# The begin of a two-layer kernel: sums of squared weights by wide products, and fewer projections ahead of the first scores

## The chip, the cores and the metric

The kernel runs on one core of one Trainium2 chip. Its time is device microseconds (us) of one execution. Three runs of the kernel before took 6031.06, 6007.41 and 6010.15 us; the median is 6010.15. A fourth execution, the one that the profile shows, took 6021.71 us.

A core has five engines with queues of their own: PE (TensorE, the matrix engine, with its weight loads shown as PEld), DVE (VectorE), ACT (ScalarE), POOL (GpSimd) and SP (SyncE, which here only issues transfers). Sixteen DMA engines move data.

## What is computed

The input x has 8 sequences of 1024 tokens with 512 values. Two residual layers follow each other. The change is in the first, modulated attention with 16 heads of 32 values:

```python
def _dcoef(weight, style):
    return rsqrt(einsum('oi,bi->bo', square(weight), square(style)) + EPS_DM)
...
x = x * s1[:, None, :]                       # s1, s2: the two halves of the styles
x = (x - mean(x)) * rsqrt(var(x) + EPS_IN)
q_dc, k_dc, v_dc = (_dcoef(w, s1) for w in (q_weight, k_weight, v_weight))
w_dc, u_dc = (_dcoef(w, s2) for w in (w_weight, u_weight))
q = heads(x @ q_weight.T * q_dc); k = heads(x @ k_weight.T * k_dc)
v_flat = x @ v_weight.T * v_dc * s2
attn = softmax(q @ k.T * d ** -0.5)
out = (attn @ heads(v_flat)) @ w_weight.T * w_dc + v_flat @ u_weight.T * u_dc
```

So each of the five weight matrices (512 x 512) needs, for each of the 8 sequences and each of 512 outputs, a factor: the root of a sum over inputs of squared weight times squared style, inverted. Only q and k factors are needed for scores; v's factor is needed for the weighing, w's and u's for the two output projections.

The second layer is a gated state-space scan over 1024 steps with 16 states for each of 1024 channels. The change touches it only in how a few tiles are allotted.

## The kernel before, in words

**Layout.** All data are float32. The attention is cut into 32 blocks: 8 sequences b by 4 groups o of four heads (128 output columns). A block has 16 slots: 8 groups of 128 queries by 2 pairs of heads. The main loop (L326 to L393) runs over the 512 slots and two more. The order of instructions on each engine is the order of the program text (`manual_schedule`); nothing is reordered by a planner, and only semaphores make engines wait for each other.

**A slot.** `scores` (L243) makes two score tiles of 128 queries by 1024 keys: for the first half of the keys from qT and kT (L252), for the second half from q2 and k2 (L255). q2 and k2 are copies of q and of the second half of k in which the upper and lower 64 partitions are exchanged (`moved`, L176: two transfers on SP's queue), so that four products run in four row strips. DVE takes the negated maximum over keys (L360), ACT the exponential with its row sum (L370), DVE the reciprocal and POOL scales the probabilities (L375, L384, L389). In the next slot PE flips them in groups of four transposes (`flip`, L262); ACT copies the flips of the first head out (L367), DVE those of the second (L381, L386). Every second slot begins with `weigh` (L269), which multiplies the flipped probabilities of the two slots before with vt, the turned v, in four column strips.

**Background.** Between these steps the slot runs a number of pieces of a generator, `background(n)`: above all `project` for the next block (for each half of the tokens: v, k, the turn of v into vt, q; each projection is a chain of four products of 128x512, L153, one piece each), the turning of the next sequence's x, and the output projections `out_w` and `out_u` of sequences and blocks already done. PIECES (L322) says how many pieces each block has to spread over its 16 slots: 42, 42, 30 and 62. Block 0 of the first sequence has no `out_w`, so it has only the 26 pieces of `project`. A second generator, `aside`, loads and normalises the next sequence's x.

**The begin.** Ahead of the main loop the text runs, in this order:
1. L104 to L110: load both halves of x of sequence 0 with their styles (`load_x`: 1 MB and 256 KB each on SP's queue), `normalise` both (POOL multiplies by the style, L72; DVE takes mean and variance, L76 and L77; ACT the root, L79; DVE the reciprocal, L80 and L81; POOL scales, L86), then `turn` both (groups of four transposes on PE, L96, copied out by ACT and DVE in turn, L98 and L100).
2. L113 to L136: for each of q, k, v, w, u load the whole matrix (1 MB, L118) into one of two buffers, square it on ACT (L119, 128x2048), and form the sums with the squared weights as the stationary operand and the 8 squared styles as the moving one (L124): 16 products with 8 moving columns for each matrix. DVE adds a constant (L131). After all five, one root (L132), one reciprocal (L133), and two more factors (L135, L136).
3. L284 to L287: load the first block's slices of the q, k and v weights, run all of `project` for block 0 (24 products and 8 transposes), and issue the loads for block 1.

PSUM gives `ps_m` two buffers (tag "mm"), shared by projections, turns, sums of squares and weighing. ACT holds one table of functions at a time; the root and the exponential are in different ones, and a load shows as ACT_TABLE_LOAD.

**After the attention**, `gated_scan` allots its tiles in the space that the attention's pools leave, loads its weights on SP's queue, and runs a plan of steps by number. `load_x1` fetches a 512 KB chunk of the first layer's result into one of two x1 buffers; `fetch` broadcasts rows from DRAM into xb buffers (256 KB each, 2048 transfers).

Of the kernel before, what the change touches and what calls it, by code (L numbers as in the profile page):

```python
# [16 lines left out]
B = 8  # L17
# [14 lines left out]
def modulated_attention(ctx, tc, const, x1_d, xu_d, S, x, xT, cond, wT, ident, sT):  # L32
# [15 lines left out]
    eps = const.tile([P, 1], F32, name="eps_h")  # L48
    nc.vector.memset(eps, EPS)
    dc = const.tile([P, 5, KH, B], F32, name="dc")  # L50
# [5 lines left out]
    def load_x(b, hf):  # L56

        xq = tok.tile([P, 4, H], F32, name="xq")
        nc.sync.dma_start(
            out=xq, in_=x[b, hf * HW : (hf + 1) * HW].rearrange("(j p) c -> p j c", p=P)  # L60
        )
        sr = tok.tile([P, H], F32, name="sr")
        nc.sync.dma_start(out=sr, in_=cond[b, 0:H].unsqueeze(0).to_broadcast([P, H]))
        return xq, sr

    def normalise(xs):
# [4 lines left out]
        for j in range(4):  # L71
            nc.gpsimd.tensor_mul(xq[:, j], xq[:, j], sr)  # L72
            yield
# [11 lines left out]
        for j in range(4):  # L85
            nc.gpsimd.tensor_scalar(xq[:, j], xq[:, j], rs[:, j, 0:1], rs[:, j, 1:2], ALU.mult, ALU.add)  # L86
            yield
# [14 lines left out]

    xh_now = []
    first = [load_x(0, 0), load_x(0, 1)]  # L104
    for xs in first:
        for _ in normalise(xs):
            pass
    for xs in first:
        for _ in turn(xs, xh_now.append):
            pass  # L110


    with tc.tile_pool(name="w0", bufs=2) as wp:  # L113
        s2T = wp.tile([P, 2 * KH, B], F32, name="s2T")
        nc.scalar.activation(s2T, sT, AF.Square)
        for n, name in enumerate(NAMES):
            w = wp.tile([P, KH, H], F32, name="w")
            nc.sync.dma_start(out=w, in_=wT[name].rearrange("(k p) o -> p k o", p=P))  # L118
            nc.scalar.activation(w, w, AF.Square)  # L119
            off = 0 if n < 3 else KH  # L120
            d_ps = ps_m.tile([P, KH, B], F32, tag="mm", name="mm_ps")
            for o in range(KH):
                for k in range(KH):
                    nc.tensor.matmul(  # L124
                        d_ps[:, o, :],
                        w[:, k, o * P : (o + 1) * P],
                        s2T[:, off + k, :],
                        start=(k == 0),
                        stop=(k == KH - 1),
                    )  # L130
            nc.vector.tensor_scalar_add(dc[:, n], d_ps, EPS_DM)  # L131
        nc.scalar.activation(dc, dc, AF.Sqrt)  # L132
        nc.vector.reciprocal(dc, dc)  # L133
    qdc, kdc, vdc, wdc, udc = (dc[:, n] for n in range(5))
    nc.vector.tensor_scalar_mul(qdc, qdc, float(HD) ** -0.5)  # L135
    nc.vector.tensor_mul(vdc, vdc, sT[:, KH : 2 * KH, :])  # L136
# [21 lines left out]

    def load_w(name, o):
# [6 lines left out]
    def project(ws, xh, b, o, st):  # L166

        qT = st["q"] = ring.tile([P, S], F32, tag="qT", name="qT")
        kT = st["k"] = ring.tile([P, S], F32, tag="kT", name="kT")
        q2 = st["q2"] = ring.tile([P, S], F32, tag="q2", name="q2")  # L170
        k2 = st["k2"] = ring.tile([P, HW], F32, tag="k2", name="k2")
        vT = st["v"] = ring.tile([P, S], F32, tag="vT", bufs=5, name="vT")
        for hf in range(2):
            c = half(hf)

            def moved(dst, src):  # L176
                nc.sync.dma_start(out=dst[64:128], in_=src[0:64])
                nc.sync.dma_start(out=dst[0:64], in_=src[64:128])
# [13 lines left out]
            for name, out in (("v", v_out), ("k", k_out), ("q", q_out)):  # L192
                yield from chain([(ws[name][:, k], xh[hf][:, k]) for k in range(KH)], out)
                if name == "k":
                    if hf == 0:
                        vt = st["vt"] = ring.tile([P, KT, P], F32, tag="vt", name="vt")
                    ps = ps_m.tile([P, 4, P], F32, tag="mm", name="mm_ps")
                    for j in range(4):
                        nc.tensor.transpose(ps[:, j], vT[:, (4 * hf + j) * P : (4 * hf + j + 1) * P], ident)
                    nc.scalar.copy(vt[:, 4 * hf : 4 * hf + 4], ps)  # L200
                    yield
# [82 lines left out]
    fetch_w(0)  # L284
    for _ in project(wts[0], xh_now, 0, 0, sts[0, 0]):
        pass
    fetch_w(1)  # L287

    def background(n):
# [5 lines left out]
        if o == KH - 1:  # L295
            w0 = load_w("u", 0)
        if o < KH - 1:
# [8 lines left out]
        fetch_w(n + 2)  # L306
        if o < 2 and b > 0:
# [18 lines left out]
    for n in range(len(slots) + 2):  # L326
# [10 lines left out]
        if bo is not None:  # L337

            done, pieces = n % SB + 1, PIECES[bo[1]]
            few = max(1, (pieces - 2 * NQ + NQ) // SB)  # L340
            due = few * (done - done // 2) + -(-(pieces - NQ * few) * (done // 2) // NQ) - ran
            ran += due
# [56 lines left out]
def gated_scan(ctx, tc, const, x1_d, S, w_in, w_conv, cols, ln_g, ln_b, w_x, w_xd, w_dt, b_dt, a_log,  # L399
# [33 lines left out]
    def load_chunk(c):  # L433
        x1 = two.tile([P, KH, B, TC], F32, name="x1")
# [10 lines left out]
    lg = load(cols["ln_g"], "lg", [P, KI])  # L445
# [544 lines left out]
```

## Time and profile before

| What | Value |
|---|---|
| Median of three runs | 6010.15 us (6007.41 to 6031.06) |
| Profiled execution | 6021.71 us |
| Its span, first to last instruction | 6019.9 us |
| Begin, to the first maximum over scores (L360) | 98.96 us |
| Block 0, from its first scores (L252) to those of block 1 | 97.74 to 199.3 us |
| Attention ends, last outputs stored (L232) | about 3464 us |
| Scan, first broadcast (L771) to the end | 3530 to 6020 us |
| PE, DVE, ACT, POOL busy | 94%, 74%, 64%, 26% |
| Mean granted TensorE clock | 0.98 of full |

"Busy" for PE is modelled from pipelined instructions; a PE that is busy may still run at a reduced clock, so the granted clock (PEclk, as a share of full speed) has to be read beside it. A product of float32 operands appears as two PE records, a transpose as one. A line of the timeline or of a table of groups names line, engine, operation, output and inputs, then how often; in brackets follows the idle time before it and what ended it. A line of the chain of waits gives start, length and what the end of the program waited for at that time.

### The profile page before, as it was taken

What the parts mean: (1) busy time and instruction counts of PE and PEld (TensorE: products, weight loads), DVE (VectorE), ACT (ScalarE), POOL (GpSimd) and SP (SyncE); (2) the same over time, 40 slices, a digit from 0 to 9 for tenths busy, and PEclk for the clock granted to TensorE, in tenths of its full rate; (3) what the DMA queues carried; (4) which work ended last, traced back from release to release, by engine and by line L of the source; (5) the groups of instructions that cost most, each with busy time, mean ns of one, the idle gap of its engine ahead of it and who ended that gap; (6) DMA issues with size and microseconds to landing.
All of it is one profiled execution on the core that took longest, in us unless ns stands there. A gap on an engine that the chain in (4) does not pass through costs nothing.

```text
span 6019.9 us, 113426 instructions
## 1 busy us (share of the span) xinstructions
PE 5660.1 (94%) x42960; PEld 3310.4 (55%) x42960; DVE 4469.2 (74%) x6917; ACT 3846.8 (64%) x6743; POOL 1549.8 (26%) x1668
## 2 busy tenths in 40 slices
PE   7999999999999999999999879999999999999998
PEld 5555555555555555555555545555555555555553
DVE  2666666766666666667666569999989998989997
ACT  3655555655655555556555358877777777777786
POOL 2433433433433434334333201101111111111111
PEclk8999999999999999999999989999999999999999
DMA  2102212111112022121111279999989999899997
GB/s 71 38 17 64 52 41 64 29 57 50 37 48 66 21 59 59 34 64 37 51 37 36 63 203 252 248 244 248 249 239 246 248 250 243 241 242 247 241 249 207
DMA packets 387648, 781.81 MB, mean 130 GB/s; under 512 B 203664, under 2 KB 285840, under 8 KB 354336
## 3 DMA queue, kind: packets, MB, share of 16 engines
q1 hardware_dynamic: 358432, 756.07, 46.2%
q0 software_dynamic: 28672, 18.48, 1.4%
q8 instruction: 342, 5.60, 0.4%
q14 instruction: 202, 1.65, 0.1%
HBM read 663.62 MB, written 83.89 MB: 124 GB/s over the span
## 4 chain that ended last, share of the span: by engine, by line
PE 51%; DMA 27%; DVE 8%; ACT 8%; SPq 4%; issue 2%; POOL 0%; ACTq 0%; DVEq 0%; POOLq 0%
DMA xb<-xd 24%; PE mm_ps L153 16%; PE t_ps L262 13%; PE s_ps L252 9%; PE mm_ps L269 8%; DVE h L805 4%; SPq L771 4%; ACT pr L370 3%; ACT pT L367 2%; PE in_ps L546 1%; DMA xd<-xt 1%; ACT xb L781 1%; DVE xt L604 1%; PE y_ps L792 1%; PE o_ps L744 1%
## 5 line engine op out<-in xcount | busy, mean ns | idle before, releaser
L360 DVE TENSOR_REDUCE nmax<-s_ps 128x1 f32<-128x1024 f32 x1024 | 1206.1, 1220 | 478.2 <-PE s_ps L255 477.6
L367 ACT COPY pT<-t_ps 128x512 f32<-128x512 f32 x1024 | 550.1, 589 | 1377.7 <-PE t_ps L262 1377.4
L805 DVE CUSTOM_DVE_ANT_0 h<-h,xb,lim 128x1024 f32<-128x1024 f32 x1024 | 1372.9, 1341 | 64.4 <-ACT xb L781 21.0
L262 PEld LDWEIGHTS t_ps<-ident,pr 128*128 128x128 f32 x8192 | 910.0, 141 | 647.0 <-issue 451.3
L781 ACT ACTIVATE xb<-xb,ws 128x1024 f32<-128x1024 f32 x1024 | 1152.4, 1146 | 174.6 <-DMA xb<-xd 151.8
L370 ACT ACTIVATE pr<-s_ps,nmax 128x1024 f32<-128x1024 f32 x1024 | 1140.3, 1128 | 5.7 <-DVE nmax L360 5.5
L262 PE MATMUL t_ps<-ident,pr 128*128 128x128 f32 x8192 | 1095.9, 277 | 30.8 <-ACT pT L367 28.5
L546 PE MATMUL in_ps<-x,win 128*128 128x256 f32 x2048 | 530.2, 405 | 88.0 <-DMA x<-x_d 88.0
L389 POOL TENSOR_SCALAR pr<-pr,rinv 128x1024 f32<-128x1024 f32 x512 | 575.2, 1123 | 144.7 <-DVE rinv L388 140.8
L252 PE MATMUL s_ps<-kT,qT 32*128 32x512 f32 x2048 | 601.0, 641 | 4.4 <-ACT pr L370 4.4
L255 PE MATMUL s_ps<-k,q 32*128 32x512 f32 x2048 | 578.0, 640 | 0.0
L759 POOL DMA_DIRECT2D out<-o_sb x256 | 150.5, 594 | 1642.5 <-ACT xr L557 824.3
L375 POOL TENSOR_SCALAR pr<-pr,rinv 128x1024 f32<-128x1024 f32 x256 | 287.5, 1123 | 1107.8 <-PE t_ps L262 740.2
L269 PEld LDWEIGHTS mm_ps<-pT,vt 128*32 128x32 f32 x16384 | 438.0, 110 | 235.3 <-issue 94.4
L269 PE MATMUL mm_ps<-pT,vt 128*32 128x128 f32 x16384 | 517.5, 274 | 47.7 <-ACT vt L200 18.6
L792 PE MATMUL y_ps<-h,yw 128*32 128x512 f32 x4096 | 533.5, 610 | 12.4 <-DVE h L805 12.4
L546 PEld LDWEIGHTS in_ps<-x,win 128*128 128x128 f32 x2048 | 397.6, 200 | 248.9 <-issue 120.1
L384 POOL TENSOR_SCALAR pr<-pr,rinv 128x1024 f32<-128x1024 f32 x256 | 287.5, 1123 | 880.8 <-DVE rinv L383 854.0
L704 PE MATMUL g_ps<-win,x1t 128*128 128x512 f32 x1024 | 467.3, 599 | 2.3 <-ACT sq_ps L630 2.3
L744 PE MATMUL o_ps<-wout,xt 128*128 128x512 f32 x1024 | 463.7, 596 | 0.1
L566 DVE SCALAR_TENSOR_TENSOR xc<-xr,cw,xc 128x256 f32<-128x256 f32 x768 | 369.5, 481 | 94.6 <-ACT xc L559 81.4
L381 DVE COPY pT<-t_ps 128x512 f32<-128x512 f32 x512 | 352.1, 688 | 77.2 <-PE t_ps L262 76.8
(131 smaller groups left out, 6830.7 us busy)
## 6 DMA issues: line engine op xcount, KB each, us to landing
xb<-xd SPq DMA_DIRECT2D x2048, 256.0 KB
xd<-xt SPq DMA_DIRECT2D x64, 512.0 KB
xq<-in_x SPq DMA_DIRECT2D x16, 1024.0 KB
q<-qT SPq DMA_DIRECT2D x128, 128.0 KB
xr<-in_xT SPq DMA_DIRECT2D x64, 256.0 KB
xu_d<-xr SPq DMA_DIRECT2D x64, 256.0 KB
xr<-xu_d SPq DMA_DIRECT2D x64, 256.0 KB
x_d<-xr SPq DMA_DIRECT2D x64, 256.0 KB
```

What stands on the lines that cost most here:

```text
L153: nc.tensor.matmul(ps, w, x, start=(k == 0), stop=(k == KH - 1))
L252: nc.tensor.matmul(s_ps[i][:, 0:HW], st["q"][r, qc], st["k"][r, 0:HW], start=True, stop=True)
L255: nc.tensor.matmul(s_ps[i][:, HW:S], st["q2"][r, qc], st["k2"][r], start=True, stop=True)
L262: nc.tensor.transpose(ps[:, j], pr[:, c0 : c0 + P], ident)
L269: nc.tensor.matmul(av[r], vt[:, kt, r], pT[:, i, kt], start=(kt == 0), stop=(kt == KT - 1), skip_group_check=True,)
L360: nc.vector.tensor_reduce(nmax[i], s_ps[i], AX.X, ALU.max, negate=True)
L367: nc.scalar.copy(pT[:, 0, 4 * g : 4 * g + 4], t_ps[g])
L370: nc.scalar.activation(fresh[i], s_ps[i], AF.Exp, bias=nmax[i], accum_out=rsum[i])
L546: nc.tensor.matmul(ps, win_sb[:, kk, k * P : (k + 1) * P], st["x1"][:, kk].rearrange("p b t -> p (b t)"), start=(kk == 0), stop=False,)
L781: nc.scalar.mul(xbs[n], xbs[n], sts[c]["ws"][:, t : t + 1])
L792: nc.tensor.matmul(st["y", i][32 * r : 32 * r + 32, hf * 512 : (hf + 1) * 512], yws[i][:, 4 * q + r, :], hs[4 * g + r][:, hf * 512 : (hf + ...
L805: nc.vector._custom_dve(dve_ops.TENSOR_ADD_SAT, out=h, in0=last["h"], in1=xbs.pop(n), s0=lim[:, 0, t : t + 1], s1=lim[:, 1, t : t + 1],)
```

## The change

It has four parts.

1. **Sums of squares.** `demod` replaces the loop at L113. For each matrix ACT squares four blocks of 128x512 one by one; the squared styles, padded with zeros to 32 columns, are now the stationary operand, and each squared block is the moving one. The four blocks' products go to four strips of 32 partitions of one PSUM tile, side by side, and are not accumulated. DVE copies the tile out, PE turns it with four transposes, and DVE reduces over the four strips (128x32) and adds the constant. Root, reciprocal and the extra factors follow for each call of `demod`.
2. **Order of the begin.** Loads: the first half of x in two parts with its style between them, the whole k matrix, the second half, the slices of k and q, the whole q matrix. Then: normalise the first half, turn it, normalise the second, `demod` of k, turn the second half, `demod` of q. Only k (both halves) and q (first half) of block 0 are projected ahead of the scores; the four squares of v's matrix are issued too. The rest of block 0's work goes into its own background: the rest of `demod` of v, projections of v, both turns of v, q's second half, then block 1's projections as before, then `demod` of w and u. In this block 56 pieces are spread, six in each of the first three slots.
3. **First normalise.** For sequence 0 the product with the style is on DVE, and two of four scalings are on ACT instead of POOL.
4. **Tiles.** The pool "w0" is gone; whole matrices use buffers of "two" (tag pT) and "tok" (tag xq). sT, eps and dc move to a pool "own" that ends with the attention. In the scan x1 has three buffers instead of two, p_add one instead of two, and the loads of lg, lb and wdt and the column of zeros use tiles that exist anyway.

```diff
 def load_x(b, hf):
     xq = tok.tile([P, 4, H], F32, name="xq")
-    nc.sync.dma_start(
-        out=xq, in_=x[b, hf * HW : (hf + 1) * HW].rearrange("(j p) c -> p j c", p=P)
-    )
+    src = x[b, hf * HW : (hf + 1) * HW].rearrange("(j p) c -> p j c", p=P)
+    if b == 0:
+        nc.sync.dma_start(out=xq[:, 0:2], in_=src[:, 0:2])
+    else:
+        nc.sync.dma_start(out=xq, in_=src)
     sr = tok.tile([P, H], F32, name="sr")
     nc.sync.dma_start(out=sr, in_=cond[b, 0:H].unsqueeze(0).to_broadcast([P, H]))
+    if b == 0:
+        nc.sync.dma_start(out=xq[:, 2:4], in_=src[:, 2:4])
...
-            nc.gpsimd.tensor_mul(xq[:, j], xq[:, j], sr)
+            (nc.vector if first else nc.gpsimd).tensor_mul(xq[:, j], xq[:, j], sr)
...
-            nc.gpsimd.tensor_scalar(xq[:, j], xq[:, j], rs[:, j, 0:1], rs[:, j, 1:2], ALU.mult, ALU.add)
+            if first and j % 2 == 0:
+                nc.scalar.activation(xq[:, j], xq[:, j], AF.Identity, bias=rs[:, j, 1:2], scale=rs[:, j, 0:1])
+            else:
+                nc.gpsimd.tensor_scalar(xq[:, j], xq[:, j], rs[:, j, 0:1], rs[:, j, 1:2], ALU.mult, ALU.add)
...
+    s2T = own.tile([P, 2 * KH, HD], F32, name="s2T")
+    nc.vector.memset(s2T, 0.0)
+    nc.scalar.activation(s2T[:, :, 0:B], sT, AF.Square)
...
+    def demod(ns, ws):
+        for n, w in zip(ns, ws):
+            for k in range(KH):
+                nc.scalar.activation(w[:, k], w[:, k], AF.Square)
+                yield
+            off = 0 if n < 3 else KH
+            d_ps = ps_m.tile([P, H], F32, tag="mm", name="mm_ps")
+            for k in range(KH):
+                nc.tensor.matmul(
+                    d_ps[k * HD : (k + 1) * HD], s2T[:, off + k], w[:, k], start=True, stop=True,
+                    skip_group_check=True,
+                )
+            nc.vector.tensor_copy(w[:, 0], d_ps)
+            yield
+            t_ps = ps_m.tile([P, KH, P], F32, tag="mm", name="mm_ps")
+            for o in range(KH):
+                nc.tensor.transpose(t_ps[:, o], w[:, 0, o * P : (o + 1) * P], ident)
+            nc.vector.tensor_reduce(
+                dc[:, n], t_ps.rearrange("p o (k m) -> p o m k", k=KH)[:, :, 0:B], AX.X, ALU.add
+            )
+            nc.vector.tensor_scalar_add(dc[:, n], dc[:, n], EPS_DM)
+            yield
+        part = dc[:, ns[0] : ns[-1] + 1]
+        nc.scalar.activation(part, part, AF.Sqrt)
+        nc.vector.reciprocal(part, part)
...
-    fetch_w(0)
-    for _ in project(wts[0], xh_now, 0, 0, sts[0, 0]):
-        pass
+    first = [load_x(0, 0)]
+    full = {"k": load_full("k", two, "pT")}
+    first.append(load_x(0, 1))
+    wts[0] = {name: load_w(name, 0) for name in "kq"}
+    full["q"] = load_full("q", two, "pT")
+    demods = {name: demod((n,), (full[name],)) for n, name in ((1, "k"), (0, "q"))}
+    for part in (
+        normalise(first[0], True), turn(first[0], xh_now.append), normalise(first[1], True), demods["k"],
+        turn(first[1], xh_now.append), demods["q"],
+    ):
+        for _ in part:
+            pass
+    wts[0]["v"] = load_w("v", 0)
+    demods["v"] = demod((2,), (load_full("v", tok, "xq"),))
+    for _ in project(wts[0], xh_now, 0, 0, sts[0, 0], (("k", 0), ("k", 1), ("q", 0))):
+        pass
+    for _ in range(KH):
+        next(demods["v"])
     fetch_w(1)
...
+        if n == 0:
+            yield from demods["v"]
+            yield from project(
+                wts[0], xh_now, 0, 0, sts[0, 0], (("v", 0), ("v", 1), ("t", 0), ("t", 1), ("q", 1))
+            )
+            rest = [load_full(name, tok, "xq") for name in "wu"]
...
         fetch_w(n + 2)
+        if n == 0:
+            yield from demod((3, 4), rest)
...
-            done, pieces = n % SB + 1, PIECES[bo[1]]
+            done, pieces = n % SB + 1, PIECES[bo[1]] if n >= SB else 56
...
+            if n < 3:
+                due = 6
+            due = max(due, 0)
...
-        x1 = two.tile([P, KH, B, TC], F32, name="x1")
+        x1 = two.tile([P, KH, B, TC], F32, bufs=3, name="x1")
...
-        add = two.tile([P, NX], F32, name="p_add")
+        add = one.tile([P, NX], F32, name="p_add")
```

## The prediction, made before the changed kernel was run

> **What bounds the kernel now.** I read the slices of the page first: TensorE is near 9 tenths in slices 2 to 23 (attention, 151 us each), and from slice 24 on the DMA engines are at 9 (the scan). The change touches the first 200 us, so I asked for the busy table of windows there.
>
> ```profile
> core 0: us, PE busy (x) PEld busy (x) DVE busy (x) ACT busy (x) POOL busy (x), PEclk, DMA share, GB/s
> 20.00:40.00 20.00, 12.74 (x64) 10.74 (x62) 6.72 (x15) 6.28 (x8) 6.85 (x8) 0.89 0.00 0
> 40.00:60.00 20.00, 19.07 (x90) 18.97 (x90) 0.39 (x2) 4.44 (x3) 0.00 (x0) 0.50 0.48 158
> 60.00:80.00 20.00, 14.25 (x48) 10.48 (x48) 1.81 (x5) 2.31 (x3) 0.00 (x0) 0.59 0.14 39
> 100.00:120.00 20.00, 15.31 (x64) 7.47 (x64) 8.55 (x15) 8.66 (x16) 4.47 (x4) 0.83 0.18 49
> ```
>
> TensorE looks busy from 40 to 60 us, but at a granted clock of 0.50 and with nothing beside it. The chain of waits (start, length, what) says what that work is.
>
> ```profile
> 9.09 4.93 POOL xq L72 x4
> 18.92 4.91 POOL xq L72 x4
> 33.66 5.42 PE mm_ps L124 x32
> 39.15 5.61 DMA w<-in_wvT
> 44.87 1.92 ACT w L119
> 46.83 7.01 PE mm_ps L124 x32
> 53.89 5.38 DMA w<-in_wuT
> 61.34 7.01 PE mm_ps L124 x32
> 69.37 3.67 DMA w_v<-in_wvT
> 73.39 8.61 PE mm_ps L153 x16
> 94.11 3.71 PE mm_ps L153 x8
> 100.94 3.61 DMA w_v<-in_wvT
> ```
>
> From 33.7 to 73.4 us everything waits for the five sums of squares (L124) and for weights that two buffers let in late; then six projection chains run before the first score; then the next block's weights are awaited, 5.81 us of idle TensorE. Last, rows of the timeline: the first maximum over scores, and the starts of the scores of four slots.
>
> ```profile
> 98.96 2.35 DVE L360 TENSOR_REDUCE nmax<-s_ps 128x1 f32<-128x1024 f32 x2 [28.53 <-PE s_ps L255]
> 147.15 0.70 PE L252 MATMUL s_ps<-kT,qT 32*128 32x512 f32 x2
> 160.15 0.70 PE L252 MATMUL s_ps<-kT,qT 32*128 32x512 f32 x2
> 171.76 0.70 PE L252 MATMUL s_ps<-kT,qT 32*128 32x512 f32 x2
> 182.96 0.70 PE L252 MATMUL s_ps<-kT,qT 32*128 32x512 f32 x2
> 263.14 1.28 ACT L79 ACT_TABLE_LOAD   x1
> ```
>
> A pair of slots without background pieces takes 182.96 - 171.76 = 11.2 us, one with about 5 pieces 160.15 - 147.15 = 13.0; in block 3 (62 pieces, 7.75 a pair) pairs are 14.7 apart (the weighings at 3316.52 and 3331.22). A piece is one 128x512 product, 0.86 us at full clock (3.60 us for the chain of four at 78.39). So in block 0 a hidden piece costs 0.35 to 0.7 us, not nothing.
>
> **Part 1: the begin, up to the first maximum (98.96 before).** I walk the new order with rows of before.
> - First half of x: 0.5 MB less lies ahead of its styles, about 1.3 us at the 390 GB/s of 9 to 15 us, so they land near 7.6 instead of 8.94; its second part near 9.0. Four DVE products of 128x512 (1.22 us for 128x1024 at L717, so 0.63) end at 10.4. Four statistics (0.69 + 0.18 + gaps) take 3.7: 14.05. Root, reciprocal and product took 15.71 - 14.96 = 0.75: 14.8. ACT and POOL now share the scaling, two each (0.57 and 0.76): 16.5. Sixteen transposes in groups of four 0.95 to 1.0 apart (copies at 29.28, 30.13, 31.07, 32.03) and the last copy: 20.6. Before, POOL alone did the products at 1.23 each.
> - Second half: its data were there by 17. DVE products 2.5, statistics 3.7, root 0.75: 27.6; scaling 28.9; four squares of the keys' weights on ACT (1.85 for 128x2048 at L119; 0.56 each) to 31.1. The four 32-wide products run in four column strips; in the scan eight such at L792 take 1.85, so four 0.93 at full clock, twice that at half. Each follows its square, so only the last shows, 0.9 to 1.8; I take 1.7 (clock half after so little work): 32.9. Copy 0.69 and hops, 33.8; four transposes 1.0, 34.8; reduction, addition and ACT's root run beside what follows.
> - Transposes of the second half: copies to 38.5 on ACT, then the queries' squares 2.3, last product 1.7, copy 0.8, transposes 1.0: 44.5. The order on TensorE puts the first projection behind this.
> - Three chains instead of six: 5.16 (the cold one at 73.39) + 3.45 + 3.45: 56.6. Evacuation 0.69 and a hop: 57.4. **A new wait:** half the score needs the moved copy q2, which is issued only now. Before, two such moves issued at 87.22 and 87.81 kept the DMA engines busy to 89.7, 2.5 us after issue; with the notice I take 3.0 (2.5 to 4): 60.4. The second half of the scores 1.15: first maximum at 61.6. Behind that wait stand in TensorE's queue the sums of squares for v and its projection; nothing else needs them yet. On SP's queue the move stands behind the whole v weights (issued when their buffer is free, at 20.6) and k2's two moves (issued some 4 us earlier), which don't hold it.
> - **Gain of part 1: 98.96 - 61.6 = 37.4 us.** Bounds: TensorE at full clock all along saves 0.8 on each of the two last products of the sums, 0.5 on their two groups of transposes, 0.2 on each of the eight groups of x and 1.7 in the first chain, about 6; later data, a cold second score (+1.2) and hops lose up to 5. So 32 to 43.
>
> The Trainium skill, "TensorE: Matmul & The Clock Gate", Part 1, speaks against the change: an idle window of about 3.4 us halves the clock and about 3.4 us of sustained work restores it. The rows agree for the idle 5.81 us before 104.69 (0.50 until 110) and for the chain at 73.39 (full after 3.3); but the clock also stayed at 0.50 from 36 to 74 us with TensorE busy on 8-column products. By the rule the 3 us for q2 keeps the clock, by the worse row it costs the first slot some 3 us.
>
> **Part 2: the first three slots.** Before, 98.96 to 122.34 = 23.4, with the 5.81 us wait (gone: the next weights are issued some 30 us ahead). After, from the first maximum: both maxima 2.35, copy 0.7, transposes 0.6; ACT's two exponentials end at 3.65, table load 1.28, root, then DVE's factors at 5.7; POOL's two scalings 1.12 each to 8.4. Beside it TensorE projects v, 3.45, to 7.2; scores 1.2; flips 1.1; three pieces 2.6; flips 1.0; v's last piece and one turn 1.5; the second turn waits for v's evacuation (14.9) to 15.5; scores 16.7; then flips 2.0, four pieces of q and two of the next block 5.3: 24.0; weighing 1.9: 25.9. **Loss 2.5 us** (0 to 6, the upper end with the half clock).
>
> **Part 3: the rest of block 0.** Before, 122.34 to 199.3 = 77.0 (its sixteenth slot ends at 199.3). After: slots 3 and 4 hold no piece, 11.4. Slots 5 to 11 hold 24 pieces, 6.9 a pair: 3.5 pairs at 14.2 = 49.6. Slots 12 to 15 hold the squares of w and u on ACT, 22.4 as empty pairs; but in slot 13 the fourth product waits for a square queued behind both exponentials, holding flips and scores some 2.7; in slot 15 the turn waits for DVE's copy behind two maxima, 1.5; and a root between exponentials costs two table loads. The trace prices that: the pair with the loads, 256.78 to 270.68, took 13.9, its twin in block 0 without them 11.6, so 2.3; here one load is half hidden, 1.8. Sum 11.4 + 49.6 + 28.4 = 89.4. **Loss 12.4 us** (6, if the 2.6 idle us of each empty pair hide all, to 18).
>
> The skill's "ScalarE: Activation LUTs", What ACT_TABLE_LOAD costs, gives 1.28 us and 1.38 of drain a switch; here the next activation starts 0.01 us after the load. With the drain the four loads would cost 5.5 us more.
>
> **What I cost at nothing.** In the scan a third x1 buffer takes ACT out of the load's wait; SP waited 0.2 us for ACT there, and TensorE's 83 us for these loads come from the filled DMA queue, where the load keeps its place. The zero column, lgb and wdt in other tiles change no order; the DMA engines (0.92 busy) hide single waits. Loads of w and u, 2 MB, are issued some eight slots ahead.
>
> **Sum.** -37.4 + 2.5 + 12.4 = -22.5 us. The profiled execution took 6021.71 (span 6019.9 and 1.8 around it), so 5999.2; the median of the runs is 11.6 lower, 6010.15, so **5987.6 us**.
>
> **Rivals.**
> - *More comes through* (5975): clock full in the begin (-6) and demodulation hidden in the empty pairs (-6). For it: 2.6 us of slack in each empty pair, four such slots. Against: transposes at 26 to 32 us ran at half pace.
> - *Most is given back in block 0* (6000): the upper ends of parts 2 and 3. For it: pieces of this trace are never free. Against: parts 1 and 3 would have to miss together.
> - *Slower* (6020): the half clock stays on after the wait for q2. A slot with six pieces holds some 9 us of TensorE work and gets up to 8 longer; from three such slots on (24 us) the gain is gone, four (32) make it 5987.6 + 32 = 6020. For it: 38 us at 0.50 before, with TensorE busy. Against: both times full chains ran, the clock was back in 3 to 6 us.
> - *The change does not do what it says*: the new order shows k and q alone ahead of the scores, so hardly.
>
> **Chances.** Forecast 0.57 (5980 to 5995), more 0.32, given back 0.07, slower 0.04. About 0.5% (30 us, 5980) is what a measurement of this kernel tells from no change, as its runs spread over 24 us: faster 0.33, within 0.63, slower 0.04. Range 5970 to 6006, from most of the second case to most of the third.
>
> **What would show it.** First maximum near 61.6 with q2 named as its wait; slot 3 about 26 us later; block 1's first score near 176; no L124-like stretch before the projections; the scan's windows unchanged. First maximum after 70 or block 1 after 190 would break the sum.

## The result, and the profile after

The changed kernel takes 5980.8 us, the median of five runs (5977.25 to 5989.09), beside 6024.03 us for the kernel before in the same series (five runs, 6007.41 to 6031.06). The ratio is 0.9941, with a 95% interval of 0.992 to 0.9963: faster by 0.4 to 0.8%. The profiled execution took 5986.2 us (span 5984.4), 35.5 us less than the profiled execution before (6021.71). The forecast was 5987.6, a gain of 22.5 us on 6010.15, the median of the first three runs of the kernel before; 5980.8 lies in its range. By the medians of this series the gain is 43.2 us, but the five runs of the kernel before spread over 24 us, so the sizes below are read from the two profiles.

The trace says where the 35.5 us come from. All three stretches of the prediction can be read from it (us):

| stretch | predicted | before | after | change |
|---|---|---|---|---|
| span's start to the first maximum | 61.6 | 98.96 | 54.87 | -44.1 (predicted -37.4) |
| first maximum to the scores of slot 3 | 25.9 | 23.4 | 24.9 | +1.5 (predicted +2.5) |
| slot 3 to the first score of block 1 | 89.4 | 77.0 | 84.6 | +7.6 (predicted +12.4) |
| sum | -22.5 | | | -35.0 |

(In the kernel before, the first products of the two heads of block 1 start apart, at 198.21 and 199.31 us. The table goes by the second, as the prediction does; by the first the sum is -33.9.)

What follows block 0 hardly moved: from there to the last store of the attention it took 3264.2 us before and 3265.8 after, and the rest of the span 2556.4 and 2554.3.

The table of windows of after, same windows and columns as for before:

```profile
core 0: us, PE busy (x) PEld busy (x) DVE busy (x) ACT busy (x) POOL busy (x), PEclk, DMA share, GB/s
20.00:40.00 20.00, 9.20 (x39) 3.67 (x40) 9.04 (x21) 7.26 (x14) 1.52 (x2) 0.74 0.15 52
40.00:60.00 20.00, 16.06 (x52) 6.60 (x51) 4.43 (x9) 9.49 (x15) 0.00 (x0) 1.00 0.25 66
60.00:80.00 20.00, 19.66 (x149) 11.02 (x151) 8.34 (x17) 11.15 (x19) 6.66 (x6) 1.00 0.09 20
100.00:120.00 20.00, 19.95 (x218) 12.20 (x217) 10.98 (x21) 10.54 (x21) 6.66 (x6) 1.00 0.07 15
```

The stretch from 40 to 80 us, which was TensorE at half clock with ScalarE at 2 to 4 of 20 us, is now projections and slots at full clock, with ScalarE and VectorE at work beside them. From 20 to 40 us TensorE is busy for less than half: there VectorE's products and statistics of the second half of x set the pace. The timeline of after, TensorE from the second half's turn to the second slot, and the first maximum:

```profile
28.23 3.47 PE L155 MATMUL mm_ps<-w,s2T 128*32 128x512 f32 x8 [9.20 <-ACT w L150]
32.48 0.66 PE L163 MATMUL mm_ps<-ident,w 128*128 128x128 f32 x4 [0.79 <-DVE w L159]
32.98 1.20 PE L107 MATMUL mm_ps<-ident,xq 128*128 128x128 f32 x8
34.48 1.15 PE L107 MATMUL mm_ps<-ident,xq 128*128 128x128 f32 x8 [0.29 <-ACT xh L109]
36.34 2.60 PE L155 MATMUL mm_ps<-w,s2T 128*32 128x512 f32 x8 [0.72 <-ACT w L150]
40.21 7.03 PE L129 MATMUL mm_ps<-xh,w_k 128*128 128x512 f32 x16
47.08 3.60 PE L129 MATMUL mm_ps<-xh,w_q 128*128 128x512 f32 x8
51.46 1.13 PE L278 MATMUL s_ps<-kT,qT 32*128 32x512 f32 x4 [0.78 <-ACT qT L206]
53.71 1.13 PE L281 MATMUL s_ps<-k,q 32*128 32x512 f32 x4 [1.12 <-DMA q<-qT]
...
54.87 2.36 DVE L414 TENSOR_REDUCE nmax<-s_ps 128x1 f32<-128x1024 f32 x2 [13.08 <-PE s_ps L281]
```

(Four products stand as eight records: "x8" is one set of sums, or one chain.) The keys' sums still run at half pace, 2.0 us behind their last square. From then on everything is at full pace: groups of transposes 0.6 to 0.7 us long, three chains in 10.5 us with no cold one. And q2's wait is there as named (L281, released by the move), 2.23 us from the issue at 51.43.

### The profile page after: what moved, and what is told of

Same layout as the page of the kernel before. It is cut to its first block, busy times and chain, and to the rows that moved or that the text cites. A ratio compares the mean times of both kernels' runs of the same rounds, so it can differ in the third digit from the quotient of the medians.

```text
span 5984.4 us, 113255 instructions
## 1 busy us (share of the span) xinstructions
PE 5632.8 (94%) x42860; PEld 3280.0 (55%) x42860; DVE 4476.6 (75%) x6938; ACT 3856.4 (64%) x6770; POOL 1533.0 (26%) x1656
## 4 chain that ended last, share of the span: by engine, by line
PE 51%; DMA 27%; DVE 8%; ACT 8%; SPq 3%; issue 2%; POOL 0%; ACTq 0%; DVEq 0%; POOLq 0%
DMA xb<-xd 22%; PE mm_ps L129 16%; PE t_ps L288 13%; PE s_ps L278 9%; PE mm_ps L295 8%; DVE h L861 5%; ACT pr L424 3%; SPq L827 3%; DMA xd<-xt 2%; ACT pT L421 2%; PE in_ps L602 1%; DMA bca<-few 1%; DMA x<-x_d 1%; ACT xb L837 1%; PE y_ps L848 1%
## 5 line engine op out<-in xcount | busy, mean ns | idle before, releaser
L281 PE MATMUL s_ps<-k,q 32*128 32x512 f32 x2048 | 577.8, 640 | 1.1 <-DMA q<-qT 1.1
L295 PE MATMUL mm_ps<-pT,vt 128*32 128x128 f32 x16384 | 519.2, 275 | 45.2 <-ACT vt L223 17.2
```

What stands on the lines that cost most here:

```text
L281: nc.tensor.matmul(s_ps[i][:, HW:S], st["q2"][r, qc], st["k2"][r], start=True, stop=True)
L295: nc.tensor.matmul(av[r], vt[:, kt, r], pT[:, i, kt], start=(kt == 0), stop=(kt == KT - 1), skip_group_check=True,)
```

## The experiments

Each changes one thing against after unless it says otherwise. Since what follows block 0 varies from run to run (block 1 to the attention's last store took 3261 to 3270 us in these traces, and the rest of the span 2536 to 2562 us, with no relation to when the attention ended), an edit of the begin is read from the trace, one profile each: at the first maximum, at slot 3 and at block 1. The runs' times where there is only one, in the order of the sections: 6007.04, 6015.25, 6004.85, 5978.55, 5993.49, 5992.94, 5980.77 and 5977.62 us.

**The sums formed as before, in the new order.** 16 products with squared weights stationary and 8 columns moving take the place of four with 512 columns.

```diff
-                d_ps[k * HD : (k + 1) * HD], s2T[:, off + k], w[:, k], start=True, stop=True,
+                d_ps[:, o], w[:, k, o * P : (o + 1) * P], s2T[:, off + k, 0:B],
+                start=(k == 0), stop=(k == KH - 1),
```

> The changed kernel with its new order, but each matrix's sums formed as before: 16 products with the squared weights as the stationary operand and 8 moving columns. The changed kernel had its first maximum over scores at 54.87 us, 6.7 earlier than worked out, and its granted clock went from 0.50 to 0.95 within 28 to 34 us, while the 512-column products of the keys' sums ran. Theory: it is these wide products that bring the clock back, so without them it stays at 0.50 until the projections; the four-transpose groups of the second half of x are 0.95 to 1.0 us apart, the first projection chain takes about 5.2 instead of 3.5, each matrix's sum some 7 us, and the first maximum comes at 62 to 68. Rival: the clock comes back with any work on TensorE after the second normalise; then the sums take about 3.5 each, the chain 3.5, and the first maximum comes at 54 to 57.

The first maximum came at 64.08. TensorE in the begin of this kernel, from its timeline:

```profile
28.87 7.28 PE L156 MATMUL mm_ps<-s2T,w 128*128 128x8 f32 x32 [9.20 <-ACT w L150]
36.00 3.85 PE L107 MATMUL mm_ps<-ident,xq 128*128 128x128 f32 x16
40.09 7.27 PE L156 MATMUL mm_ps<-s2T,w 128*128 128x8 f32 x32 [0.24 <-ACT w L150]
47.21 9.26 PE L129 MATMUL mm_ps<-xh,w_k 128*128 128x512 f32 x16
56.31 3.60 PE L129 MATMUL mm_ps<-xh,w_q 128*128 128x512 f32 x8
...
69.76 6.49 PE L129 MATMUL mm_ps<-xh,w_v 128*128 128x512 f32 x8
```

The sums last as long as before the change (7.00 for 32 records at the granted clock of 0.50), and what stands behind them is slow too: the transposes take 0.96 us a group, two key chains 9.26 instead of 7.03. The chain for q is at full pace again (3.60), and the first chain of v, behind the narrow sums for v, takes 6.49 (3.60 in after, 4.9 to 5.3 in five other profiles with the wide form, see below). That is what my working had assumed for the new form. By its column this profile grants full clock from 25 to 60 us; the durations say otherwise, so it is the pace that is to be read there. The same happens in slots 12 to 15, where the sums for w and u lie: the second slot of block 1 starts at 196.22 instead of 171.54.

**The new form alone, in the old order** (this edits the kernel before; its loads still pass through two buffers).

```diff
-            nc.scalar.activation(w, w, AF.Square)
+            for k in range(KH):
+                nc.scalar.activation(w[:, k], w[:, k], AF.Square)
+                nc.tensor.matmul(
+                    d_ps[k * HD : (k + 1) * HD], s2T[:, off + k], w[:, k], start=True, stop=True,
```

> The kernel before with only the form of the sums changed (blocks squared one by one, moving weights in four strips, copy, four transposes, reduction), all five still in a row ahead of the projections. Theory: the form alone is worth the shorter sums and the clock, but the loads through two buffers (5.4 to 5.6 us each in the chain of before) still set the pace for v, w and u, so the first maximum moves from 98.96 only to 84 to 90. Rival: the sums were the bound and the loads hide, so it comes below 80; other rival: the loads set everything, so it stays above 94.

First maximum 92.83, 6.1 us earlier than before: between the two expectations. The five sums now start at 33.6, 38.4, 44.9, 50.2 and 56.7 us, and the loads of wv and wu, 5.6 us each, stand in the chain of waits; the sums for q, v and u last 3.5 us, at half pace again after a wait, those for k 1.06.

**All of block 0 projected ahead of the scores**, with v's factors.

```diff
+    for _ in demods["v"]:
+        pass
-    for _ in project(wts[0], xh_now, 0, 0, sts[0, 0], (("k", 0), ("k", 1), ("q", 0))):
+    for _ in project(wts[0], xh_now, 0, 0, sts[0, 0]):
```

> The changed kernel with the factors of v and all of block 0's projections ahead of the scores again (24 products instead of 12), w's and u's sums still in block 0's background. Theory: the deferred products are paid back almost in full in block 0, since TensorE is what block 0 waits for: the first maximum comes 12 to 15 us later (67 to 70), block 0 gets shorter by nearly as much, and block 1's first scores come at 165 to 168 instead of 164.4. Rival: block 0 hides the deferred work, so deferring it is most of the gain: block 1's first scores come at 172 or later.

First maximum 72.10, 17.2 us later than after; the second slot of block 1 starts 13.3 us later, at 184.80. So the rival held: postponing v and half of q is worth most of what it takes out of the begin. Not all of that is hidden work, for the old wait for the next weights returns in this kernel's timeline, and 6.27 us of its block 0 go there:

```profile
78.29 3.41 PE L129 MATMUL mm_ps<-xh,w_v 128*128 128x512 f32 x4 [6.27 <-DMA w_v<-in_wvT]
```

These three set side by side, at the start of block 1's second slot:

| form of the sums | order of loads and halves | v and half of q | us | against before |
|---|---|---|---|---|
| old | old | ahead | 205.97 | |
| new | old | ahead | 199.91 | -6.1 |
| old | new | postponed | 196.22 | -9.8 |
| new | new | ahead | 184.80 | -21.2 |
| new | new | postponed | 171.54 | -34.4 |

The form alone and the order with the postponing alone add up to 15.9 us; together they give 34.4.

**The first normalisation on GpSimd, as before.**

```diff
-        normalise(first[0], True), turn(first[0], xh_now.append), normalise(first[1], True), demods["k"],
+        normalise(first[0]), turn(first[0], xh_now.append), normalise(first[1]), demods["k"],
```

> The changed kernel with the first normalise as before: the products with the style and all four scalings on POOL. Theory from the rows of both traces: POOL's products (1.23 each) of the second half run while TensorE turns the first, so its statistics end some 2 us earlier, ACT is free for the keys' squares earlier, and the first maximum comes no later than 54.9, about 50 to 53. Rival: POOL is the slow engine of the begin, as the chain of before showed, and the split over DVE and ACT saves its 4 us: the first maximum comes at 57 or later.

First maximum 52.58, so up to there this part of the change costs 2.3 us. The second half's factors come no earlier (VectorE's last step of them begins at 25.62, in after at 25.94), but ScalarE, which now scales nothing, squares the keys' weights sooner: their first product starts at 25.94 instead of 28.23, and GpSimd's scaling lies beside the sums. Block 1 began no earlier for it (165.34 against 164.36), as the clock was lost in two slots of this run: in slot 0 (12.1 us to the next slot instead of 10.4) and in slot 13 (9.7 instead of 8.1), where it falls to 0.50 behind a wait of 2.51 us for a square.

**The scan's tiles as before** (x1 with two buffers, p_add in the pool with two).

```diff
-        x1 = two.tile([P, KH, B, TC], F32, bufs=3, name="x1")
+        x1 = two.tile([P, KH, B, TC], F32, name="x1")
-        add = one.tile([P, NX], F32, name="p_add")
+        add = two.tile([P, NX], F32, name="p_add")
```

> The two edits in the scan that could cost or bring time are undone (x1 with two buffers, p_add in the pool with two); the begin and block 0 are as after. Theory (the scan part of the change is worth nothing): 5975 to 5992 us, and the stretch from the first product of the scan to the end is within 3 us of that of after. Rival (part of the 35 us came from a third x1 buffer): over 6000.

From the last store of the attention to the end it took 2554.9 us against 2554.3. These two edits show no effect, as costed; but that stretch took 2536 to 2562 us in these traces, so one run can't show a small one, and the other edits of tiles weren't tried by themselves. The attention, which is the same code, took 6.7 us longer than in after's profile. 2.1 of them lie in slot 0, in this kernel's timeline:

```profile
55.20 1.42 PE L155 MATMUL mm_ps<-w,s2T 128*32 128x512 f32 x8
58.31 1.12 PE L163 MATMUL mm_ps<-ident,w 128*128 128x128 f32 x4 [1.69 <-DVE w L159]
59.22 5.29 PE L129 MATMUL mm_ps<-xh,w_v 128*128 128x512 f32 x8
```

The granted clock falls to 0.50 at about 56 us and is back at 62: v's first chain takes 5.29 instead of 3.60. Of the six profiles with this slot 0 behind three chains (after's and five of its variants), five lost the clock there (chains of 4.9 to 5.3) and only after's kept it; the three with the folded begin below kept it.

**The first slot's scores without the moved copies.**

```diff
+                elif st is sts[0, 0] and q == 0 and pair == 0:
+                    r = slice(64 * pair + i * HD, 64 * pair + (i + 1) * HD)
+                    nc.tensor.matmul(s_ps[i][:, HW:S], st["q"][r, qc], st["k"][r, HW:S], start=True, stop=True)
```

> The first slot's second half of the scores is made from qT and kT themselves, in the same row strips as its first half, so it doesn't wait for the moved copies q2 and k2; all else is as after. Theory (the wait for the move is in the path of the first maximum and nothing else is late behind it): in the trace of after TensorE stood idle 1.12 us before L281, between 52.59 and 53.71, so the first maximum comes at 53.7 to 54.0 instead of 54.87, and the whole run is about 1 us shorter. Rival (the two halves in one pair of strips take turns, or the exponentials wait for something else): first maximum at 54.5 or later. My prediction had put this wait at 3.0 us from issue to release; the trace of after shows 2.2.

By its number the rival: first maximum 54.88. But the first score already began 1.4 us late (52.86), because the clock came back later in this run (the second turn took 3.81 in one piece, from 33.68). From the first score to the maximum it took 2.02 us instead of 3.41, so the wait is gone. v's first chain was slow here too (4.85): the clock is also lost without the wait for q2.

**Eight pieces more behind the slots of block 0** (the next block's q chains done twice).

```diff
+            if n == 0:
+                yield from project(wts[1], xh_now, 0, 1, sts[0, 1], (("q", 0), ("q", 1)))
```

> Eight pieces more in the background of block 0 (the two chains for q of the next block are done a second time, with their evacuations and moves; the pieces of the block go from 56 to 64): the price of a hidden piece, measured by itself. Theory from the trace of after: slots 5 to 11 with 24 pieces took 46.9 us, 3.5 pairs, where empty pairs take 11.2, so 0.32 us a piece, and the stretch from slot 3 to the first score of block 1 grows by 2.0 to 3.5 us, from 84.6 to about 87. Rival, my prediction's price (0.35 to 0.7 a piece): 87.4 to 90.2. Rival, TensorE is the bound and nothing is hidden (0.86 a piece): 91.5.

All expectations missed: from slot 3 (81.94) to block 1 (177.02) it took 95.1 us, 10.5 more than 84.6. Slots 5 to 11 hold 29 pieces instead of 24 and took 52.0 instead of 46.9: 1.0 us for each added piece, with its share of evacuations and moves. The other three lie in slots 4 and 12, which grew by 0.7 us together; slot 13 grew by 1.0 without a piece. So the price isn't one number: up to 6.9 pieces a pair the mean is (13.4 - 11.2) / 6.9 = 0.32 us, and what comes on top costs as much as TensorE needs for it (0.86) and a little more. Another 3.7 us arose in slot 15, where the shifted sum for u now waits for a square behind both exponentials, at a table load, and where the granted clock falls to 0.50 behind that wait (from 175 us); in its timeline:

```profile
172.65 1.28 ACT L170 ACT_TABLE_LOAD   x1
172.68 1.04 PE L155 MATMUL mm_ps<-w,s2T 128*32 128x512 f32 x2 [2.51 <-ACT w L150]
```

**The fourth square of w a slot earlier.** After has that same wait in slot 13; its timeline:

```profile
145.97 1.06 PE L155 MATMUL mm_ps<-w,s2T 128*32 128x512 f32 x6
149.54 1.05 PE L155 MATMUL mm_ps<-w,s2T 128*32 128x512 f32 x2 [2.51 <-ACT w L150]
...
151.98 0.70 PE L278 MATMUL s_ps<-kT,qT 32*128 32x512 f32 x2
```

```diff
+            if n == 3:
+                yield
...
+            if n == 12:
+                due += 1
```

> As after, but the fourth square of w is issued in slot 12, behind that slot's own exponentials, and no longer in slot 13 behind slot 13's; the order of the products on TensorE is the same. Theory (in the trace of after TensorE stands idle 2.51 us in slot 13 for that square alone): the wait goes, slot 13 takes 5.4 to 6.2 us instead of 8.1, and the stretch from slot 3 to the first score of block 1 takes 81.8 to 83.5 us instead of 84.6. Rival (the slot waits for its maxima and exponentials anyway): slot 13 stays at 7.5 us or more.

The same place in this kernel, in its timeline:

```profile
149.51 1.06 PE L157 MATMUL mm_ps<-w,s2T 128*32 128x512 f32 x8
...
152.86 0.70 PE L280 MATMUL s_ps<-kT,qT 32*128 32x512 f32 x2
```

The sums run in one piece, slot 13 takes 5.4 us (147.42 to 152.86) instead of 8.1, and slot 3 to block 1 takes 82.0 instead of 84.6. The theory held.

**The begin folded, in three steps.** The idle time that after shows from 20 to 28 us on TensorE and ScalarE is filled: the keys' sums go ahead of all transposes, the first key projection ahead of the second half's turn; sums use the PSUM buffers of the flips. ScalarE alone copies the turned first half, the first slot has the direct scores of the run above, and in block 0 a piece stands between a matrix's last square and its product.

```diff
+    for part, count in (
+        (n0, 8), (nk, 4), (n0, 5), (n1, 4), (nk, 2), (t0, 2), (nk, 1), (n1, 2), (nk, 1), (n1, 2), (t0, 3),
+        (nk, 2), (nq, 1), (n1, 1), (nq, 1), (n1, 4), (nq, 2), (lv, 1), (pk0, 5), (t1, 5), (nq, 2), (pk1, 5),
+        (nq, 4), (pq0, 5),
+    ):
+        for _ in range(count):
+            next(part, None)
```

(n, t and p are normalising, turning and projecting, nk and nq the sums for k and q in pieces, lv the loads for v.)

> A new order of the begin, built on what the trace of after shows idle there. TensorE and ScalarE stand still from 19.7 to 26 us while VectorE normalises the second half of x. Here the keys' weights are squared and summed before the first transposes, the products and statistics of the second half run on VectorE while ScalarE alone copies the turned first half, the first projection of keys comes before the second half is turned, and the sums for q lie between the key projections; the first slot's scores need no moved copy; in block 0 one piece more is put between the last square and its product. Theory (the order of the begin sets the first maximum, and TensorE runs at full clock): with data of the weights there by 12 us, first maximum at 37 to 42 us instead of 54.87, slot 13 loses its 3 us of waiting, and the run takes 5962 to 5972 us. Rival (half clock through the begin, since so little work precedes the projections): first maximum at 43 to 48 and 5970 to 5980. Rival (the first slots wait for v's weights or their squares, which don't come earlier): first maximum early, but slot 3 no earlier than 72, and the run over 5975.

First maximum 41.66, inside the theory's range, and block 1 at 150.14; the run took 5972.5 us, just above the theory's 5972 (median of four, 5965.04 to 5995.9), ratio 0.9929 with 0.9902 to 0.9957. The first half is turned late. One reason is a table load of 1.28 us ahead of its root (at 14.07), the other shows in the timeline on GpSimd:

```profile
16.19 3.35 POOL L97 TENSOR_SCALAR xq<-xq,rs 128x512 f32<-128x512 f32 x2 [15.73 <-DMA w_q<-in_wqT]
25.16 1.52 POOL L97 TENSOR_SCALAR xq<-xq,rs 128x512 f32<-128x512 f32 x2 [5.62 <-DVE rs L89]
```

The same two scalings take 3.35 us beside VectorE's products and 1.52 without them. The second step gives this work to VectorE and brings the root's table in early:

```diff
+    nc.scalar.activation(warm, eps, AF.Sqrt)
-                nc.gpsimd.tensor_scalar(xq[:, j], xq[:, j], rs[:, j, 0:1], rs[:, j, 1:2], ALU.mult, ALU.add)
+                (nc.vector if first else nc.gpsimd).tensor_scalar(
```

> The folded begin once more, with two edits against what its trace shows late there. A root of one column right after the first square brings the root's table in while ScalarE has nothing to do, so that the 1.28 us load at 14.07 doesn't stand between the statistics and the root; and VectorE does half of the scaling in place of GpSimd, whose two scalings took 3.35 us beside VectorE's products, against 1.52 without them. The transposes for the keys' factors come after the whole first half is turned. Theory (these two set when the first half is turned, and TensorE is the bound from there): the first half turned some 3 us earlier, first maximum at 37 to 40 us instead of 41.66, block 1 at 145 to 149, the run 5955 to 5972. Rival (the second half's statistics on VectorE become the bound, since VectorE now also scales): first maximum at 40.5 or later and no gain over the folded begin. Against before, both: ratio 0.989 to 0.993.

The rival's number, 41.46, though only in part by its mechanism: TensorE waits 1.38 us at 24.11 for the scaled second half, and longer for something else. The first projection started at 19.12 instead of 23.30, but the gain was lost behind it, on ScalarE and TensorE in its timeline:

```profile
24.67 1.65 ACT L152 ACTIVATE w<-w 128x512 f32<-128x512 f32 x3
26.23 0.67 ACT L246 ACTIVATE kT<-mm_ps,dc 128x512 f32<-128x512 f32 x1
...
26.95 3.02 PE L109 MATMUL mm_ps<-ident,xq 128*128 128x128 f32 x12 [1.69 <-ACT kT L246]
```

The projection's evacuation stands behind three squares, and the second half's transposes wait for its PSUM buffer. The run: 5968.85 (median of five), ratio 0.992 with 0.9905 to 0.9936. The third step moves the evacuation ahead of these squares, and takes in the earlier square of w:

```diff
-        (nq, 1), (n1, 5), (nq, 3), (lv, 1), (pk0, 5), (t1, 5), (nq, 2), (pk1, 5),
+        (nq, 1), (n1, 5), (lv, 1), (pk0, 5), (t1, 1), (nq, 1), (t1, 1), (nq, 1), (t1, 1), (nq, 1), (t1, 2),
+        (nq, 2), (pk1, 5),
```

> The tightened begin with one edit: the evacuation of the first projection of keys stands on ScalarE ahead of the last three squares of the queries' weights, which come between the copies of the turned second half; block 0 has its fourth square of w a slot earlier. In the begin before it the projection was done at 22.7, its evacuation began only at 26.23 behind these squares, and the second half's transposes stood still until 26.95 for it. Theory (that queue on ScalarE was the bound): the second half is turned some 2 us earlier, first maximum at 38.5 to 40 instead of 41.46, and the run some 2 us, with the square some 4 us, shorter than the tightened begin; ratio against before 0.990 to 0.9935. Rival (the sums for q now come later, since their squares do, and hold the second projection of keys): first maximum at 41 or later.

First maximum 39.16, block 1 at 146.00, the attention's last store at 3409.69 (3430.13 in after). The run: 5967.6 us (median of four, 5966.01 to 5972.99), ratio 0.991 with 0.9886 to 0.9934. In the trace the attention ends 20.4 us earlier than in after's. By the times alone this kernel isn't separated from after, since the intervals of their ratios overlap, nor from the second step (5968.85), where 4 us less were expected; the scan happened to take 2561.5 us in this profile.

## Why the prediction was right, and where its sizes were off

The three steps of the sum were the right ones, each with the right sign. By the median what came out lies in the forecast's 5980 to 5995, at its edge; by the trace it has the number of the second case ("more comes through", 5975): 6010.15 - 35.0 = 5975.2. I gave that case 0.32 and the forecast 0.57. That the number fits so well is luck, since of the case's two conditions one held in part and one didn't: the clock brought nearly 4 of its 6 us, but the demodulation wasn't hidden. Slots 12 to 15 took 26.5 us, where four empty ones take 22.4. The rest came from other terms.

**Part 1 was mis-sized by 6.7 us, nearly 4 of them by one term: the clock.** I took "clock half after so little work", groups of 0.95 to 1.0 and a cold chain of 5.16, from rows of before. In after only the first sums ran at half pace (2.0 behind their last square where I had 1.7: +0.3). The second turn took from 32.98 to 35.6 instead of four groups of 1.0 (-1.3), the queries' sums end 1.1 behind their last square (-0.6), the transposes of both sums take 0.66 instead of 1.0 (-0.6), and the three chains 10.5 instead of 12.05 (-1.6). q2 took 2.2 instead of 3.0 (-0.8), and the second half began earlier (VectorE turned to it at 19.7, and I had 20.6: -0.9); where the rest, 1.2, lies wasn't read off.

The term that was mis-sized rests on a transfer of those rows. In the timeline of before each of them stands behind a wait of some 5 us, the transposes ahead of any 8-column product:

```profile
25.62 2.87 PE L96 MATMUL mm_ps<-ident,xq 128*128 128x128 f32 x11 [5.32 <-ACT xh L98]
...
73.39 5.16 PE L153 MATMUL mm_ps<-xh,w_v 128*128 128x512 f32 x8 [5.06 <-DMA w_v<-in_wvT]
```

The new form in the old order, which has no narrow products, has such a cold chain at the same place too, in its timeline:

```profile
66.40 6.03 PE L157 MATMUL mm_ps<-xh,w_v 128*128 128x512 f32 x8 [4.74 <-DMA w_v<-in_wvT]
```

In after only the keys' sums stand behind a long wait (9.20 us). From there to the first score TensorE never waits more than 0.8 us, and the half pace ended with these sums. The run with the old form shows that the kind of work in this place counts as well: with 8-column products the pace stays half, through 7.28 us of sums, 3.85 of transposes and the chain behind. So the new form is worth more than the products it saves. The trace of before held the one side of this, the stretch at 0.50 with TensorE busy; I cited it, and then costed as if it were a matter of how much work had been done.

Part of it was luck. In three of seven profiles with this begin the second turn took 3.4 to 3.8 us instead of 2.65. One of them is the run with the earlier square, the same code up to slot 12: its first maximum came at 56.27, which would make part 1 mis-sized by 5.3 instead of 6.7.

**Part 2 held** (24.9 against 25.9), but by luck of the clock. The half clock that I gave as its upper end came in five of the six profiles named above, which took 26.6 to 27.0 us, and stayed for one slot; the sixth is after. So the "slower" rival names a real mechanism with too high a price: it ends with the first chain.

**Part 3 was mis-sized by 4.8 us.** Slots 5 to 11 took 46.9 instead of 49.6, slots 12 to 15 took 26.5 instead of 28.4. The wait in slot 13 was right in place and size: "some 2.7", and the run without it shows 2.66. Slot 15 took 6.3 us. The two table loads I had at 1.8 cost about 0.5, in block 1, where its first slot takes 7.18 us instead of 6.67 (from 199.31 in before):

```profile
163.18 1.28 ACT L170 ACT_TABLE_LOAD   x1
164.48 0.26 ACT L170 ACTIVATE dc<-dc 128x64 f32<-128x64 f32 x1
...
167.21 1.28 ACT L424 ACT_TABLE_LOAD   x1
```

On ScalarE of after, the loads stand before a root that nothing in the slot needs, and before exponentials whose maxima come at that time. As to hidden pieces, my rows gave 0.36 and 0.45 us, and the upper end of "0.35 to 0.7 us" had none. The range is also wrong in kind: up to 6.9 a pair they cost 0.32, and further ones 1.0, more than their full time.

**What I costed at nothing** in the scan shows nothing, as far as one run can tell. Moving the first normalisation to VectorE and ScalarE, which I had counted within the gain, by itself delays the first maximum by 2.3 us.

Open remains why the clock is lost in slot 0 in some executions and kept in others of the same code; no run here was made to tell.

## What to carry to other kernels

Before a chain is costed with a row from elsewhere, look at what ran ahead of that row: a duration carries with it the clock that the wait and the work ahead of it have left, and an edit that changes these changes the row. Two halves of a change can be worth twice their sum (here 34.4 us beside 15.9) when each is held up by what the other removes, so a part tried alone can look weak. Work hidden behind slots has a price that rises: measure the slack once, by adding pieces until the slots grow by their full length.

## What the runs showed of the hardware

Narrow products did not raise the clock in these runs, and in before it fell under them. The first 8-column products there follow each other every 0.11 us, from 33.66 to 35.4 us, and all later ones every 0.21. The table of windows of before shows it, with 18 records in two us and then 11 (columns as in the first table):

```profile
34.00:36.00 2.00, 2.00 (x18) 2.00 (x17) 0.00 (x0) 1.41 (x1) 0.00 (x0) 0.86 0.00 0
36.00:38.00 2.00, 2.00 (x11) 2.00 (x11) 0.00 (x0) 0.00 (x0) 0.00 (x0) 0.50 0.00 0
```

The granted clock then stood at 0.50 until 70 us with TensorE busy up to 100%, while behind one set of four 512-column products in after, at half pace for 3.5 us, everything ran at full pace. That isn't certain either: in seven profiles with this begin the second turn ran at full pace in four, and took 3.4 to 3.8 us instead of 2.65 in three. Which trait of the narrow products keeps the clock down isn't shown: they have few columns, and weight loads beside them all the time (PEld 18.97 of 20 us from 40 to 60). The rule in the Trainium skill, "TensorE: Matmul & The Clock Gate", Part 1, that some 3.4 us of sustained work are enough, agrees with the wide products in four of these seven profiles and not with the narrow ones. The same part warns that clock events in a trace can be unreliable; the run with the old form shows it, with a column at 1.00 beside products of 0.23 us that take as long (0.22) at 0.50 in before.

GpSimd's two scalings took 3.35 us beside VectorE's two-input products and 1.52 beside none. In after the same two took 1.51 beside none, at 14.43, with the DMA engines as busy as in the slow case, so these aren't the reason. The Trainium skill, "GPSIMD Engine Reference", Specifications, says of the memory interface that it is shared with VectorE and that instructions with two inputs there contend; the run agrees, and puts a price on it, 1.8 us for two tiles.
